# A state-space scan on one core: the product with C written over the states, decays sent three units ahead, and the scan's waits gathered on one instruction

## The chip, the core and the metric

The program runs on one core of a Trainium2 chip. Its engines run side by side, each from its own queue and in that queue's order: PE (TensorE, matrix products), DVE (VectorE), ACT (ScalarE), POOL (GpSimd) and SP (SyncE, which here only issues transfers). The metric is the device time of one execution in microseconds.

## The reference

The reference is two layers. The first adds to x an attention with small latents and a gated feed-forward. The second adds a selective scan (a state-space layer) and a low-rank expert layer. The change lies in the selective scan. For each of 4 sequences of 256 steps, 1024 channels and 16 states per channel:

```python
def step(h, inp):
    x_t, dt_t, B_t, C_t = inp
    dA = jnp.exp(dt_t[..., None] * A)
    dBx = dt_t[..., None] * B_t[:, None, :] * x_t[..., None]
    h = dA * h + dBx
    y = jnp.einsum('bdn,bn->bd', h, C_t)
    return (h, y)
...
y = (ys + D_param[None, :, None] * xc) * jax.nn.silu(z)
return jnp.einsum('bdl,hd->blh', y, out_proj_w)
```

x, z, dt, B and C come from projections of the layer's normalized input, x through a short convolution and a silu, dt through a softplus.

## The kernel before, in words

The order of the work is written out by hand: the program's text is the order of each engine's queue, and a table `put(b, s, f)` says in which unit of the scan a piece of other work is sent. Waits between engines are added from the tiles that instructions read and write.

The first layer takes the first 330 us or so, and its last products (`down`, L469) run on PE until 349.8 us beside the first units of the scan. From there on the scan sets the rhythm. It has 4 batches (stage 0 to 3) of 8 channel blocks of 128 channels, and each block is done in 4 units, one for every 4 of the 16 states: 128 units, numbered `u`. A unit's tiles are [128, 4, 256]: 32 channels by 4 states on the partitions, 4 groups of channels and 256 steps along the free axis. The steps of a unit are:

- `decays(u)`, ACT, L982: four exponentials, exp(dt * A), into a decay tile. There are three such tiles besides the lent ones; unit u takes tile (u - 4) mod 3. They are sent in unit u - 2, at the head of that unit's work on ACT. The tile that they write was last read by the scan of unit u - 3, which is the unit before the one in which they are sent.
- `scan_in(u)`, DVE, L989 and L993: from unit 8 on a no-operation that carries waits (for the decays of u and for POOL's product of u - 2), then bx = B * (dt * x) into PSUM.
- `scan(u)`, DVE, L1008: the recurrence along the steps, into a tile h; then on POOL, L1013, hc = h * C into a tile hc. There are two h tiles and three hc tiles. The first four units use lent tiles (`lent`, L961) in the place of later ones.
- `states_sum(u)`, PE, L1023 and L1025: eight passes that sum hc over the states into ysum. It is sent at the end of unit u + 1, behind that unit's other products on PE. At the end of a block, `take_sum` on ACT (L1030) copies ysum out, and `gate` on POOL (L1033) multiplies it with silu(z).

dt and dt*x reach the layout of the unit through DRAM: POOL makes them (`step_out`, L916 to L920; `step_x`, L927), `send` (L935) stores them, and `spread` (L941) loads them back with four transfers each, as dts for the decays and dus for bx. All of these transfers are on SP's queue, in the text's order, with the weight loads (L623).

The other work of a stage prepares the next batch and ends the one before: on PE the projections px (L759) and pz (L950), the convolution's products (L806), pp (L833), the output products po (L1121) and others; on ACT the copies and scalings of the convolution, two large silu with their table loads (L822, L956, L710), the logarithms and exponentials of dt (`step_exp`, L886 to L889), the inverse root for B, C and dt (L714, L715) and, in two of the stages, ex for the routing (L1070); on DVE a scaling of pp (nrm, L847), statistics, and the routing (from L1060); on POOL the products named above and the sums of the convolution (L813). In unit 4 ACT also does a silu of z (L956) and the scaling of the next batch (xnt, L735), which PE transposes (L743).

## Time and profile before

| what | value |
| --- | --- |
| median of 3 runs | 840.59 us (839.35 to 841.75) |
| the profiled execution's own time | 840.18 us |
| its span | 838.4 us |
| TensorE clock granted, mean | 0.953 |
| busy: PE, DVE, ACT, POOL | 750.9, 654.6, 554.2, 496.9 us |
| decays (L982), one of four | 501 ns, 504 of them |
| hc (L1013) | 2324 ns, 130 of them |
| scan (L1008) | 2235 ns, 129 of them |
| bx (L993) | 1232 ns, 128 of them |

The mean of a row mixes its shapes; the full-sized scan has a median of 2286 ns and the full-sized hc one of 2358 ns. In the trace, "idle before" is the time for which an engine had nothing to do ahead of an instruction, and the name after it is what ended that wait. A wait for several things is put down to the one that came last by the profile. PE's ends are modelled. In the lines of a timeline the columns are start, duration, engine, line and operation, then output and inputs with their sizes.

### The profile page before, as it was taken

To read this page: it belongs to the slowest core of one execution; us is meant where nothing else is said; L and a number is where in the kernel's file an instruction comes from. 1 tells how busy PE (TensorE), PEld (TensorE's weight loads), DVE (VectorE), ACT (ScalarE), POOL (GpSimd) and SP (SyncE) were. 2 spreads that over 40 slices of the span, in tenths; PEclk is the share of its full clock that TensorE was granted. 3 is DMA by queue.
4 is the path that set the end of the run, shared out by engine and by line. 5 is a ranking of instruction groups with operands and counts; after the bars stand their busy time and mean duration, and the time that the engine had idled before them with its cause. 6 is when DMAs were issued, how large, how long until landed. Compare 5 with 4: busy or idle time off the path is not lost.

```text
span 838.4 us, 11286 instructions
## 1 busy us (share of the span) xinstructions
PE 750.9 (90%) x3846; PEld 429.6 (51%) x3846; DVE 654.6 (78%) x604; ACT 554.2 (66%) x1124; POOL 496.9 (59%) x389
## 2 busy tenths in 40 slices
PE   4999999999999999999887999897899987876985
PEld 2665545666555676666543456444457544322331
DVE  4486756288644535797899999988999999999996
ACT  4335564435556277699895898687898787865661
POOL 3133232001343333678878799769799769798775
PEclk9799999999999999999999899989999989988898
DMA  7233332001222322454593544433554443443400
GB/s 226 63 101 106 96 101 63 1 1 38 76 76 79 115 57 64 149 141 126 130 217 109 160 150 115 126 91 105 144 165 114 112 110 92 119 114 120 113 26 25
DMA packets 68644, 86.72 MB, mean 103 GB/s; under 512 B 12221, under 2 KB 52169, under 8 KB 68458
## 3 DMA queue, kind: packets, MB, share of 16 engines
q1 hardware_dynamic: 58794, 65.81, 29.0%
q0 software_dynamic: 9072, 18.35, 7.8%
q10 hardware_dynamic: 720, 1.84, 0.6%
q8 instruction: 30, 0.49, 0.3%
q14 instruction: 28, 0.23, 0.1%
HBM read 66.58 MB, written 10.22 MB: 92 GB/s over the span
## 4 chain that ended last, share of the span: by engine, by line
PE 45%; DVE 23%; POOL 12%; ACT 9%; issue 5%; DMA 5%; SPq 1%; POOLq 0%; ACTq 0%; DVEq 0%
DVE h L1008 11%; POOL hc L1013 8%; PE pg L444 6%; DVE bx L993 6%; PE pu L444 5%; PE po L469 5%; PE av L397 4%; ACT decay L982 3%; PE po L1121 2%; PE px L759 2%; DMA dus<-dud 2%; PE scT L386 2%; DVE mpl L354 2%; PE ysum L1025 2%; DMA dts<-dtd 2%
## 5 line engine op out<-in xcount | busy, mean ns | idle before, releaser
L1013 POOL TENSOR_TENSOR hc<-h,cr 128x1024 f32<-128x1024 f32 (+1 forms) x130 | 301.9, 2324 | 80.5 <-DVE h L1008 70.4
L1008 DVE TENSOR_TENSOR_SCAN h<-decay,bx 128x1024 f32<-128x1024 f32 (+1 forms) x129 | 288.1, 2235 | 8.5 <-PE po L469 3.6
L982 ACT ACTIVATE decay<-dts,aneg 128x255 f32<-128x255 f32 x504 | 213.6, 501 | 52.8 <-DVE h L1008 38.2
L993 DVE TENSOR_TENSOR bx<-brow,dus 128x1024 f32<-128x1024 f32 x128 | 157.7, 1232 | 24.2 <-ACT decay L982 9.3
L1025 PE MATMUL ysum<-hc,stack 128*32 128x256 f32 x1024 | 88.4, 417 | 39.3 <-POOL hc L1013 39.3
L456 POOL TENSOR_TENSOR hlo<-g,hhi 128x512 fp32r<-128x512 f32 x28 | 35.8, 1280 | 115.0 <-ACT hhi L455 115.0
L354 DVE TENSOR_REDUCE mpl<-sc 128x4 f32<-128x1024 f32 x64 | 76.7, 1220 | 22.8 <-PE sc L352 21.3
L427 POOL DMA_DIRECT2D wgu<-in_wgu x56 | 31.1, 555 | 96.0 <-PE pg L444 95.0
L388 ACT ACTIVATE pe<-scT 128x1024 f32<-128x1024 f32 x64 | 64.0, 1023 | 22.9 <-PE sc L352 14.3
L1121 PE MATMUL po<-ow,xc 128*128 128x512 f32 x128 | 72.4, 671 | 5.3 <-POOL xc L1033 4.9
L1025 PEld LDWEIGHTS ysum<-hc,stack 128*32 128x32 f32 x1024 | 21.2, 111 | 99.1 <-POOL hc L1013 69.7
L950 PE MATMUL pz<-xn1T,w_in 128*128 128x256 f32 x256 | 69.3, 419 | 0.0
L759 PE MATMUL px<-xn1T,w_in 128*128 128x256 f32 x256 | 61.0, 383 | 0.4 <-ACT sz L956 0.3
L950 PEld LDWEIGHTS pz<-xn1T,w_in 128*128 128x128 f32 x256 | 50.2, 205 | 19.8 <-issue 11.6
L759 PEld LDWEIGHTS px<-xn1T,w_in 128*128 128x128 f32 x256 | 47.5, 190 | 13.1 <-issue 3.1
L452 DVE SCALAR_TENSOR_TENSOR g<-g,pg 128x512 f32<-128x512 f32 x28 | 19.2, 687 | 43.0 <-ACT g L451 43.0
L444 PE MATMUL pg<-xhi,wgu 128*128 128x512 f32 x112 | 49.7, 443 | 1.0 <-ACT xhi L244 1.0
L469 PE MATMUL po<-wd,hhi 128*128 128x512 f32 x112 | 49.2, 439 | 0.0
L444 PE MATMUL pu<-xhi,wgu 128*128 128x512 f32 x112 | 47.5, 424 | 0.8 <-DVE g L454 0.8
L455 ACT CAST hhi<-g 128x512 fp32r<-128x512 f32 x28 | 17.3, 619 | 45.8 <-DVE g L454 45.8
L444 PE MATMUL pg<-xlo,wgu 128*128 128x512 f32 x112 | 44.9, 401 | 0.7 <-DVE xlo L251 0.7
L444 PE MATMUL pu<-xlo,wgu 128*128 128x512 f32 x112 | 44.6, 398 | 0.0
(237 smaller groups left out, 1276.8 us busy)
## 6 DMA issues: line engine op xcount, KB each, us to landing
dts<-dtd SPq DMA_DIRECT2D x124, 128.0 KB, 2.8
dus<-dud SPq DMA_DIRECT2D x124, 128.0 KB, 3.0
wgu<-in_wgu POOLq DMA_DIRECT2D x56, 256.0 KB, 2.7
w_in<-in_inz SPq DMA_DIRECT2D x16, 512.0 KB, 4.7
w_in<-in_inx SPq DMA_DIRECT2D x14, 512.0 KB, 4.4
dtd<-dt SPq DMA_DIRECT2D x15, 256.0 KB, 2.3
dud<-du SPq DMA_DIRECT2D x15, 256.0 KB, 2.3
wd<-in_wd POOLq DMA_DIRECT2D x7, 512.0 KB, 3.5
```

Of the source, the lines that this page charges most:

```text
L354: nc.vector.tensor_reduce(mpl2[b % 2][:, qb, 2 * hp : 2 * hp + 2, 16 + 2 * gq : 18 + 2 * gq], sc.rearrange("p i (f k) -> p i f k", f=2), A ...
L388: nc.scalar.activation(pes[b, k][:, 2 * t : 2 * t + 2, :], sc, AF.Exp)
L444: mm(ps, lhsT=wgus[i][:, hc, :], rhs=xs[j][:, hc, :], start=(hc == 0 and j == 0), stop=(hc == HC - 1 and j == 1))
L469: mm(po, lhsT=hids[th][j][:, m, i * P : (i + 1) * P], rhs=wd[:, m, :], start=False, stop=(m == MC - 1 and j == 1))
L759: mm(px[:, i, :], lhsT=w[:, i, hc, :], rhs=xns[b][:, hc, :], start=(hc == 0), stop=(hc == HC - 1))
L950: mm(pz[:, i, :], lhsT=w[:, i, hc, :], rhs=xns[b][:, hc, :], start=(hc == 0), stop=(hc == HC - 1))
L982: made["da", u] = nc.scalar.activation(da[:, k, 1:], live["dts", b, c][:, k, 1:], AF.Exp, scale=aneg[:, c, k, g : g + 1])
L993: nc.vector.tensor_tensor(bx, brow[g // 2][:, g % 2, :].unsqueeze(1).to_broadcast([P, NG, S]), live["dus", b, c], ALU.mult)
L1008: nc.vector.tensor_tensor_scan(h[:, n].rearrange("p n t -> p (n t)"), da[:, n].rearrange("p n t -> p (n t)"), bx[:, n].rearrange("p n t -> ...
L1013: made["hc", u] = (nc.vector if k == NG - 1 else nc.gpsimd).tensor_tensor(hc[:, n], h[:, n], crows[b][:, g, :].unsqueeze(1).to_broadcast([ ...
L1025: mm(ysum[k * NB : (k + 1) * NB, :], lhsT=stack, rhs=hc[:, k, :], start=False, stop=(g == NU - 1))
L1121: mm(live["po", b, i], lhsT=xcs[b][:, c, i * P : (i + 1) * P], rhs=late_w["ow"][:, c, :], start=False, stop=(c == DC - 1))
```

## The change

It has three parts.

1. POOL's product with C is written over h, and the hc tiles are gone: four h tiles in the place of two h and three hc. The no-operation ahead of bx waits for the product of unit u - 4 and for PE's sum of unit u - 4, where it waited for the product of unit u - 2. The tiles lent to the first four units are fewer.
2. There are four decay tiles besides the lent ones where there were three, and the decays of a unit are sent three units ahead of it where it was two. The first unit of a batch stays two ahead, and nothing is sent by the new rule before unit 3: units 5 and 6 are both sent in unit 3, unit 7 in unit 4.
3. The no-operation of the first unit of each block also waits for the four transfers of dus, for which bx itself waited.

```diff
-        for i in range(NG):
-            nc.sync.dma_start(t[i * NB : (i + 1) * NB], src)
+        made[n, b, c] = [nc.sync.dma_start(t[i * NB : (i + 1) * NB], src) for i in range(NG)]
...
-    lent = {
-        "d": ("d", "w_in", "d", "w_in"), "h": ("w_in", "u", "e", "u"),
-        "hc": ("w_in", "lw", "w_in", "lw"),
-    }
+    lent = {"d": ("d", "w_in", "d", "w_in"), "h": ("w_in", "lw", "e", "u")}
+    ahead = 3
...
-            da = decay[(u - 4) % 3]
+            da = decay[(u - 4) % (ahead + 1)]
...
             i = nc.vector.engine_nop()
-            for n in (("da", u), ("hc", u - 2)):
-                tc.add_manual_dep(i.ins, made[n].ins.name, early, reason="the scan's waits")
+            first = made["du", b, c] if g == 0 else []
+            for j in (*first, made["da", u], made["hc", u - 4], made["sum", u - 4]):
+                tc.add_manual_dep(i.ins, j.ins.name, early, reason="the scan's waits")
...
-            h, hc = lend("h", u), lend("hc", u)
+            h = lend("h", u)
         else:
-            h = act.tile([P, NG, S], F32, tag="h", name="h", bufs=2)
-            hc = act.tile([P, NG, S], F32, tag="hc", name="hc", bufs=3)
+            h = act.tile([P, NG, S], F32, tag="h", name="h", bufs=4)
...
             made["hc", u] = (nc.vector if k == NG - 1 else nc.gpsimd).tensor_tensor(
-                hc[:, n], h[:, n],
+                h[:, n], h[:, n],
...
-        live["hc", u] = hc
+        live["hc", u] = h
...
-            mm(ysum[k * NB : (k + 1) * NB, :], lhsT=stack, rhs=hc[:, k, :],
-               start=False, stop=(g == NU - 1))
+            made["sum", u] = mm(ysum[k * NB : (k + 1) * NB, :], lhsT=stack, rhs=hc[:, k, :],
+                                start=False, stop=(g == NU - 1))
...
-        decay_tile(act)
-        decay_tile(act)
+        for _ in range(ahead):
+            decay_tile(act)
...
+    due = {}
+    for v in range(5, total):
+        due.setdefault(max(v - ahead + (v % PER == 0), 3), []).append(v)
     for u in range(total + 2):
...
-        if 3 <= u < total - 2:
-            decays(u + 2)
+        for v in due.get(u, ()):
+            decays(v)
```

## The prediction

> **What bounds the kernel now.** I read the stretches first (engine totals for the four batches), then VectorE's waits, the rows of the scan's four steps, and last the timelines of all engines around each wait. Stage b is batch b of the scan: units 32b to 32b+31, a unit being bx, scan, hc and ysum of one quarter of the states. Unit numbers count the L993 rows from the first one at 327.42 us.

> Stretches of the kernel before (per engine: busy us and instructions):

> ```profile
> 327.00:467.00 140.00, 122.55 (x655) 77.66 (x654) 122.97 (x102) 114.57 (x259) 108.99 (x71) 0.94 0.59 150
> 467.00:591.00 124.00, 112.09 (x566) 60.95 (x567) 113.87 (x70) 101.44 (x231) 103.51 (x63) 0.94 0.44 122
> 591.00:715.00 124.00, 112.23 (x596) 63.09 (x594) 117.45 (x90) 102.38 (x234) 103.28 (x62) 0.97 0.43 121
> 715.00:840.00 125.00, 94.83 (x430) 36.20 (x426) 114.01 (x71) 71.67 (x154) 92.80 (x52) 0.89 0.30 83
> ```

> VectorE (the third figure of busy time) leads, but PE, ACT and POOL are at 82 to 91% in the first three stages, so a stall of VectorE is often only the shadow of another engine that is full. VectorE's own waits from 327 us on (total us, times, longest):

> ```profile
> DVE bx L993 <- ACT decay L982: 9.3, 8, 4.1
> DVE bx L993 <- POOL hc L1013: 6.7, 10, 1.1
> DVE h L1008 <- PE po L469: 3.6, 1, 3.6
> DVE bx L993 <- ACT pad L771: 3.2, 1, 3.2
> ```

> The last one, at unit 16, is POOL's too: ACT's copy was long done, and hc of unit 14 ended 0.24 us before that bx. Floor of a unit, from the rows of page part 5: bx 1.232 + scan 2.286 + two gaps of 0.035 = 3.59 us. Over the 128 units, gaps before bx sum to 28.3 us, of which the floor is 5 and some 3 lie around small VectorE work; the removable waits are 9.1 (decays, eight times) and 10.4 (POOL, unit 16 and seven small ones included): 19.5 us.

> [...] the ten POOL waits are for h, which has two. [...] where the nop let go late, bx came 0.20 us after hc's end and not 0.04. [...]

> **The change, part by part.**

> *C in place, four h.* Five tiles become four. POOL's product in place: the halves L918 (in place) and L927 (not) both took 1.27 us, so 0; at most the row's own spread, 40 ns for each of some eight products in a POOL-bound end, 0.3 us either way. The nop's wait for hc(u-2) becomes hc(u-4), which every hc in the trace meets (the latest ended 7.8 us after its scan; 10.8 are allowed). Added is PE's ysum(u-4). Behind the waiting nop stands all of VectorE; POOL and PE wait for that. It must be done three units and a gap after its scan: 3 x 3.59 + 0.04 = 10.8 us. Latest ysums now: unit 17 at 10.97, 49 at 10.53, 13 at 10.38, 88 at 9.70. PE is late there by its own queue, so each microsecond that VectorE gains before comes back here.

> *Decays three ahead.* No instruction is added; a group of four (1.65 us) enters ACT's queue one unit earlier and still waits for scan(u-1). So, in time, each ACT slot keeps its place and holds the next unit's group: 3.6 us more margin once the queue is running. dts must land a slot earlier: the least margin by slot is 0.1 us (unit 16) and -0.2 (unit 24), with VectorE not waiting there; at the batch starts the order stays two ahead. To get ahead, one extra group is put in at unit 4:

> ```profile
> 349.86 3.30 ACT L982 ACTIVATE decay<-dts,aneg 128x255 f32<-128x255 f32 x8 [7.28 <-PE po L469]
> 353.18 1.28 ACT L956 ACT_TABLE_LOAD   x1
> ```

> ```profile
> 357.25 1.82 PE L743 MATMUL pt<-cst,xnt 128*128 128x128 f32 x8 [1.92 <-ACT xnt L735]
> ```

> The program's order has twelve decays where these eight stand. ACT then has 0.2 us idle until 402.9, and PE waits only for ACT (1.9, 1.0, 0.3, 0.5). So both run 1.65 us later up to the silu near 410 us and the product behind it. Bounds: 0 (absorbed) to 1.65; I take 1.65. The one added clearing on POOL is 0.1 us, under PE's po.

> *dus waits on the nop.* Four DMA waits per channel block move ahead one instruction. They were exposed only where POOL held the nop (0.16 x 6 = 1 us, counted in the 10.4); alone the part is worth 0 to 1 us, I take 0 beside the first. The previous scan (2.29 us) covers them on VectorE's queue; uncovered they would cost 0.16 at 31 block starts, 5 us. The SP queue keeps its order.

> *Loans in units 0 to 3.* Two fewer w_in tiles are lent, so SP's weight loads near 347 to 361 us may go sooner; no px or pz in that stretch waits for a load, so 0. Late, they would hold px, but they can only be earlier.

> **Stage by stage.**

> *Stage 0.* Up to unit 20 the waits go (10, 13, 14, 16), but VectorE runs into ysum and into dus(20), which POOL's full queue sends. Deciding are:

> ```profile
> 417.14 0.64 PE L1025 MATMUL ysum<-hc,stack 128*32 128x256 f32 x8
> ```

> ```profile
> 418.89 0.42 ACT L715 ACTIVATE rs<-rs 64x256 f32<-64x256 f32 x1
> ```

> ```profile
> 419.38 1.23 DVE L993 TENSOR_TENSOR bx<-brow,dus 128x1024 f32<-128x1024 f32 x1
> ```

> This ysum (17) ends at 417.8 + 1.65 = 419.4 and releases bx(21), which started at 419.38 anyway. rs ends at 419.3 + 1.65 = 420.96; nrm (0.47) and the scan follow at 421.4, against 420.9 before: 0.5 lost. POOL's wait at unit 29 goes: +0.8. Stage 0: +0.25 of the 9 us of stalls.

> *Stage 1.* The wait at 38 goes (0.74) and POOL, which idled 0.72 for that scan, moves with it; PE idles 0.79 for POOL at 507 us and follows. After that PE and POOL have no hole until 531 us, so the waits at 43 to 51 (1.5 us) end in ysum(49) at 543.4 - 0.7 and nrm at unit 53; the gain stands at 0.74. Then the largest wait:

> ```profile
> 567.16 1.23 DVE L993 TENSOR_TENSOR bx<-brow,dus 128x1024 f32<-128x1024 f32 x1 [4.12 <-ACT decay L982]
> ```

> ```profile
> 557.23 1.70 ACT L982 ACTIVATE decay<-dts,aneg 128x255 f32<-128x255 f32 x4
> ...
> 565.33 1.70 ACT L982 ACTIVATE decay<-dts,aneg 128x255 f32<-128x255 f32 x4
> ```

> Unit 58's group moves into the slot at 557.2, 59's into 565.3. bx(59) can start at 567.0 - 0.7 + 0.1 = 566.4 against 570.75: gain 4.35; the wait at 61 makes it 5.15. POOL is full from 561.8 (waiting for ACT) with one hole of 0.72, so it moves by 0.74 + 0.72 = 1.46, and dus(64), landed at 588.38, by as much: bx(64) at 587.0 against 591.17. Stage 1: +4.1.

> *Stage 2.* Waits of 2.65 us in all, but the routing at unit 89 starts when ACT's ex lands:

> ```profile
> 684.09 0.20 DVE L1060 TENSOR_REDUCE w<-ex 128x4 f32<-128x32 f32 x1 [0.83 <-ACT ex L1070]
> ```

> ACT and PE move only by the 0.24 of unit 70, so 0.25 is left there. After it unit 93 (0.77) and 96 (0.14) go: +1.2.

> *Stage 3.* VectorE alone, 115 of 115 us; 0.38 at unit 102 and 0.08 at 112 go: +0.5. The tail is unchanged.

> Sum 0.25 + 4.1 + 1.2 + 0.5 = 6.0 us. The profiled execution took 840.18 (span 838.4 and 1.8 around it), so 834.2; the median shown is 0.4 higher, and I say 834.3.

> **The rivals.**

> *All stalls go* (chance 0.06): 19.5 us, 820.7. For it: every stall named is addressed. Against: PE has no hole in 507 to 531 us, ACT none in 350 to 403.

> *The opening push is absorbed and the full queues yield* (0.22): stage 0 gains 1.5 + 0.8, stage 1 the 5.15, stage 2 its 2.65, stage 3 0.5: 10.6 us, 829.6. For it: PE's ends are modelled, so its holes may be larger than shown. Against: rs and ex are ACT's, not modelled.

> *The gains are eaten, within 0.3%* (0.12): bx(59) waits, because ACT's slots after unit 55 hold one group more than I count (1.65, and its push on POOL 1.0), stage 2 gives 0.3 and stage 3 nothing: 0.25 + 1.45 + 0.3 = 2.0 us, 838.2, or 838.6 beside the median. For it: ACT is full from 557 to 574 us. Against: the slot count above.

> *PE's ysum becomes the pace* (0.05), slower. At units 30, 62 and 94 two groups stand in one unit. If that pushes PE by 1.65 each time as at unit 4, lags are 12.6, 12.2 and 11.3 us in stages 0 to 2; past the allowed 10.8 every excess (1.8, 1.4, 0.6) is lost, and what the other waits give back is spent waiting: 840.2 + 3.8 = 844. It decides where a lag passes 10.8 us and VectorE has no other stall to trade. Against: the unit before has no group, so ACT's slots only swap.

> That the decays are not earlier can't be: the program's order has them so.

> **How the numbers follow.** The likeliest (0.55) is 834.3, its own range 831.5 to 837. The 80% range is 827.5 to 839: it leaves out the first rival, the fastest tail of the second, and the slower one. A measurement tells about 0.3% (2.5 us) from no change; below 838.1 is faster: 0.55 + 0.22 + 0.06 = 0.83. Within 0.3%: 0.12. Slower: 0.05.

> **What would show it.** Right: no wait of bx for POOL's hc; bx waiting for PE's ysum at units 17 and 21 (1 to 2 us each) and at 53; dus a wait at 20 and 64; unit 58 free and 59 waiting under 1.5 us for ACT; twelve decays in a row near 350 us and the transposes of xnt 1.65 us later; stage 1 shorter by 4 us, stage 0 by less than 1. Wrong: ysum waits over 3 us in sum, stage 0 shorter by 2 or more, or ACT still ahead of bx at 58.

## The result, and the profile after

| | kernel before | changed kernel |
| --- | --- | --- |
| median | 840.66 us (839.35 to 842.86, 8 runs) | 837.25 us (835.19 to 838.26, 8 runs) |
| ratio to before, 95% interval | | 0.9952 (0.9940 to 0.9965) |
| profiled execution, its span | 840.18, 838.4 us | 836.09, 834.3 us |
| start of the first bx | 327.42 us | 324.83 us |
| TensorE clock granted, mean | 0.953 | 0.952 |

The kernel is faster by 3.4 us; 6.0 to 6.3 were forecast. In a second series it was 836.35 us against 840.70, ratio 0.9947 (0.9931 to 0.9962).

Below "gain" always counts from the bx of unit 0: the start of a step minus the start of bx of unit 0, kernel before less the other. That is needed because the two heads, in which nothing was changed, differ by 2.6 us; over the thirteen profiles of this study the first bx started at 324.8 to 327.6 us.

VectorE's waits in the scan of the changed kernel (total us, times, longest):

```profile
DVE bx L991 <- PE ysum L1022: 5.4, 5, 2.4
DVE bx L991 <- POOL xc L1030: 3.8, 1, 3.8
DVE h L1005 <- PE po L469: 3.6, 1, 3.6
DVE bx L991 <- POOL h L1010: 2.6, 1, 2.6
DVE w L1057 <- ACT ex L1067: 2.5, 1, 2.5
DVE nrm L847 <- ACT rs L715: 2.4, 2, 1.2
...
DVE bx L991 <- ACT decay L979: 1.7, 1, 1.7
...
DVE bx L991 <- DMA dus<-dud: 1.3, 2, 0.9
```

The removable waits of before, ACT's decays and POOL's hc, are gone. In their place stand PE's sums, dus and the two ends of ACT's chains, rs and ex: the queues that were full all along. Three names mislead: the 3.8 at unit 20 is dus (the second profile names its transfer, 3.6 us); the 2.6 at unit 53 is the sum of unit 49, which ended 0.20 us before that bx (the second profile: ysum, 2.3 us); and the 1.7 at unit 13 is the sum of unit 9, which ended 0.20 us before that bx, when the decays had been done for 2.6 us.

The large wait of stage 1 is where the gain is made. In the kernel before, unit 58 waited 4.12 us. These are bx and scan of unit 58 and bx of unit 59 in the changed kernel, and then bx of unit 64, with which stage 2 begins:

```profile
562.26 1.23 DVE L991 TENSOR_TENSOR bx<-brow,dus 128x1024 f32<-128x1024 f32 x1
563.53 2.29 DVE L1005 TENSOR_TENSOR_SCAN h<-decay,bx 128x1024 f32<-128x1024 f32 x1
565.85 1.23 DVE L991 TENSOR_TENSOR bx<-brow,dus 128x1024 f32<-128x1024 f32 x1
...
586.25 1.23 DVE L991 TENSOR_TENSOR bx<-brow,dus 128x1024 f32<-128x1024 f32 x1 [0.90 <-DMA dus<-dud]
```

By stages the gain, from two profiles of the changed kernel against the first of before (stage 3 up to the end of the span):

| stage | forecast | measured, profile 1 and 2 |
| --- | --- | --- |
| 0 | +0.25 | -1.07, -1.23 |
| 1 | +4.1 | +3.40, +3.62 |
| 2 | +1.2 | -1.26, -0.23 |
| 3 | +0.5 | +0.43, +0.36 |
| sum | 6.0 | 1.5, 2.5 |

The kernel before, profiled again, took 1.0 us more for its scan than in its first profile, so 1.5 to 3.6 us is what the profiles of the scan give; the medians give 3.4 and 4.4.

Stage 0 goes wrong at its start. First ACT's push of decays, then PE beside it, in the changed kernel:

```profile
347.26 4.90 ACT L979 ACTIVATE decay<-dts,aneg 128x255 f32<-128x255 f32 x12 [7.34 <-PE po L469]
352.18 1.28 ACT L955 ACT_TABLE_LOAD   x1
```

```profile
356.25 1.97 PE L743 MATMUL pt<-cst,xnt 128*128 128x128 f32 x8 [3.52 <-ACT xnt L735]
...
360.02 2.07 PE L872 MATMUL pdt<-nrm,dtw 32*128 32x256 f32 x4
...
363.03 3.10 PE L759 MATMUL px<-xn1T,w_in 128*128 128x256 f32 x8
```

Twelve decays stand in a row, and the transposes of xnt wait 3.52 us where they waited 1.92: the forecast push of 1.65 us (measured 1.60 on ACT). Not forecast are the last two lines: products of a size that take 1.13 and 1.99 us elsewhere took 2.07 and 3.10. The stretches of 3.4 us show why; the seventh figure is PE's granted clock (us, then PE, PEld, DVE, ACT and POOL busy, clock, DMA share, GB/s):

```profile
351.50:354.90 3.40, 1.24 (x8) 0.66 (x4) 3.12 (x3) 3.35 (x5) 1.31 (x2) 1.00 0.82 191
...
358.30:361.70 3.40, 3.40 (x14) 1.42 (x13) 3.27 (x2) 3.40 (x10) 2.87 (x2) 0.50 0.43 134
361.70:365.10 3.40, 3.40 (x14) 1.92 (x14) 3.33 (x3) 3.40 (x10) 2.36 (x1) 0.50 0.54 140
365.10:368.50 3.40, 3.40 (x22) 2.34 (x21) 3.33 (x3) 3.34 (x5) 2.38 (x1) 0.97 0.00 0
```

In the records of the clock it is at half from 355.1 to 365.3 us, 10.2 us; in the kernel before this took 3.4 us (357.8 to 361.2). My theory after this, then untested: the push costs 1.6 us by its length and nearly as much again by PE's clock, and clock losses in stages 1 and 2 take more. The rivals: the sum of u-4 and dus are the limit and the push is harmless; or the push counts, but the clock doesn't.

### The profile page after: what moved, and what is told of

It is laid out like the page before. It is cut to its first block, busy times and chain, and to the rows that moved or that the text cites. A ratio compares the mean times of both kernels' runs of the same rounds, so it can differ in the third digit from the quotient of the medians.

```text
span 834.3 us, 11274 instructions
## 1 busy us (share of the span) xinstructions
PE 749.0 (90%) x3846; PEld 429.7 (51%) x3846; DVE 654.7 (78%) x604; ACT 554.0 (66%) x1124; POOL 496.9 (60%) x390
## 3 DMA queue, kind: packets, MB, share of 16 engines
q10 hardware_dynamic: 720, 1.84, 0.7%
## 4 chain that ended last, share of the span: by engine, by line
PE 47%; DVE 26%; ACT 9%; POOL 7%; issue 5%; DMA 4%; SPq 1%; ACTq 0%; POOLq 0%; DVEq 0%
DVE h L1005 13%; DVE bx L991 7%; PE pg L444 6%; PE pu L444 5%; PE px L759 4%; POOL h L1010 4%; PE av L397 4%; PE px L806 3%; PE po L469 3%; PE ysum L1022 3%; PE scT L386 2%; PE po L1118 2%; PE pz L949 2%; PE pp L833 2%; ACT decay L979 2%
## 5 line engine op out<-in xcount | busy, mean ns | idle before, releaser
L1010 POOL TENSOR_TENSOR h<-h,cr 128x1024 f32<-128x1024 f32 (+1 forms) x130 | 302.0, 2326 | 72.3 <-DVE h L1005 60.5
L991 DVE TENSOR_TENSOR bx<-brow,dus 128x1024 f32<-128x1024 f32 x128 | 157.7, 1232 | 19.0 <-PE ysum L1022 5.4
L1022 PE MATMUL ysum<-h,stack 128*32 128x256 f32 x1024 | 87.0, 412 | 37.9 <-POOL h L1010 37.9
L1022 PEld LDWEIGHTS ysum<-h,stack 128*32 128x32 f32 x1024 | 21.0, 111 | 97.3 <-POOL h L1010 66.2
L469 PE MATMUL po<-wd,hhi 128*128 128x512 f32 x112 | 49.2, 439 | 0.0
```

Of the source, the lines that this page charges most:

```text
L469: mm(po, lhsT=hids[th][j][:, m, i * P : (i + 1) * P], rhs=wd[:, m, :], start=False, stop=(m == MC - 1 and j == 1))
L991: nc.vector.tensor_tensor(bx, brow[g // 2][:, g % 2, :].unsqueeze(1).to_broadcast([P, NG, S]), live["dus", b, c], ALU.mult)
L1010: made["hc", u] = (nc.vector if k == NG - 1 else nc.gpsimd).tensor_tensor(h[:, n], h[:, n], crows[b][:, g, :].unsqueeze(1).to_broadcast([P ...
L1022: made["sum", u] = mm(ysum[k * NB : (k + 1) * NB, :], lhsT=stack, rhs=hc[:, k, :], start=False, stop=(g == NU - 1))
```

## The experiments

The gain over the first profile of before, at the bx of the units named, with the half clock (us) in three places: after the push (units 4 to 11), at pp (units 16 to 21), and around unit 50 (from 1 us ahead of bx of 49 to bx of 54).

| kernel | u22 | u32 | u52 | u54 | u64 | u84 | u89 | u127 | half clock: push, pp, u50 |
| --- | --- | --- | --- | --- | --- | --- | --- | --- | --- |
| before, 2nd profile | -0.54 | -0.53 | -0.69 | -0.70 | -0.30 | -0.31 | -0.32 | -1.04 | 3.4, 3.4, 3.4 |
| changed | -1.84 | -1.07 | 1.18 | -1.79 | 2.33 | 4.25 | 0.22 | 1.55 | 10.2, 3.4, 6.8 |
| changed, 2nd profile | -1.99 | -1.23 | 1.02 | -1.71 | 2.39 | 4.31 | 1.32 | 2.64 | 10.2, 3.4, 6.8 |
| product_only | 0.01 | 0.75 | 1.17 | 1.16 | 1.99 | 1.83 | 1.82 | 1.28 | 3.4, 3.4, 3.4 |
| decays_only | -0.43 | -0.45 | 0.62 | -0.63 | 0.80 | 1.77 | 0.77 | 1.30 | 3.4, 3.4, 3.4 |
| late_lead | 0.18 | 0.91 | 3.16 | 3.23 | 6.97 | 8.89 | 6.43 | 7.76 | 3.4, 3.4, 0 |
| early_dus | 0.19 | 0.92 | 3.16 | 0.75 | 4.70 | 6.62 | 4.10 | 5.43 | 3.4, 3.4, 3.4 |
| warm_pe | -1.60 | -0.83 | 1.42 | -0.02 | 3.65 | 4.35 | 0.75 | 2.08 | 0, 6.8, 3.4 |
| warm_both | -1.80 | -1.05 | 1.19 | -1.59 | 2.59 | 4.50 | 1.41 | 2.73 | 0, 0, 6.8 |
| warm_short | -0.91 | -0.15 | 2.10 | -0.75 | 3.34 | 5.26 | 2.23 | 3.56 | 3.4, 0, 6.8 |
| stage0_order | 2.38 | 3.13 | 5.38 | 3.87 | 7.71 | 9.63 | 7.11 | 8.43 | 3.4, 3.4, 3.4 |
| all_order | 2.60 | 3.35 | 5.60 | 4.91 | 6.85 | 8.77 | 4.65 | 5.98 | 3.4, 3.4, 6.8 |

### The two kernels again

Labels after_again and before_again, no edit.

> The changed kernel once more, beside the others on one chip. Both theories: 837.2 us, 0.995 of the kernel before, stage 0 (bx of unit 0 to bx of unit 32) 140 us, with some 10 us of half clock on PE right after unit 4.

> The kernel before once more, for how far one profiled execution stands for others. Theory (stages repeat, and what differs between executions is where PE's clock halves): stage 0 138.5 to 139.3 us, stage 1 124 to 125.5, stage 2 123 to 124.5, stage 3 123.7, each longer where there is more half clock; bx of unit 0 at 324.8 to 327.6 us. Rival (one profile tells nothing of others): stages differ by 2 us or more with the same stretches of half clock.

Measured: 836.35 us (835.88 to 837.85), ratio 0.9947 (0.9931 to 0.9962), stage 0 140.19 us, half clock 10.2 us after the push; and, before again, 839.38 us in one run, stages 139.49, 124.56, 123.53 and 124.45 us (the first 0.2 and the last 0.7 us over what I expected), first bx at 325.57. Units repeat to some 0.2 us where the clock's stretches lie alike, and differ by 1 us where they don't: at unit 89, 0.22 with 9.9 us of half clock since unit 85 and 1.32 with none. So a gain at a unit can be compared between profiles, if the clock is read beside it.

### No push at the opening

Label late_lead: the lead of three begins at unit 30.

```diff
-        due.setdefault(max(v - ahead + (v % PER == 0), 3), []).append(v)
+        due.setdefault(v - 2 if v < 30 else v - ahead + (v % PER == 0), []).append(v)
```

> The changed kernel, but the lead of three units begins only at unit 30 (units below that are sent two units ahead), so that no third group of decays stands in the queue of ACT at unit 4. Theory (the opening push idles PE for 3.5 us ahead of the transposes of xnt, PE's clock goes to half for 10 us, and stage 0 loses both): stage 0 takes 136.8 to 137.5 us in place of 140.0, half clock after unit 4 at most 3.4 us, time 834.2 to 834.8. Rival 1 (stage 0 lost its gain to the new wait for the sum of u-4 and to dus, not to the push): stage 0 139.5 to 140, time 837. Rival 2 (only the 1.65 us of the push count, not the clock): stage 0 138.4, time 835.6.

Measured: stage 0 138.04 us, half clock after unit 4 3.4 us, 836.46 us (832.18 to 838.00), ratio 0.9942 (0.9921 to 0.9963). Stage 0 is 2.0 us shorter than the changed kernel's, so the push does harm, and rival 1 falls. But it is not as short as I expected (136.8 to 137.5), and it lies nearer to rival 2 (138.4, the push without the clock), so this run doesn't tell the two apart. At unit 20 VectorE waits about as long as in the changed kernel (3.84 us there), now for the decays, which at a lead of two come late.

```profile
415.73 1.23 DVE L991 TENSOR_TENSOR bx<-brow,dus 128x1024 f32<-128x1024 f32 x1 [4.05 <-ACT decay L979]
```

The median is no better than the changed kernel's 836.35. Here and in early_dus, which has the same waits in stage 0, five executions of thirteen had a mean clock of 0.954 or more, and took 832.2 to 834.7 us; the other eight took 835.0 to 838.0. Of the fourteen executions of the changed kernel one reached 0.954, and the fastest took 835.19 us. So in these runs what is won over the changed kernel shows only where PE's clock stays up.

### Is it PE's clock?

Labels warm_pe, warm_both and warm_short: products whose results are overwritten, in PE's idle time ahead of the transposes of xnt, and (in the last two) ahead of pp.

```diff
         pt = psmm.tile([P, HC, P], F32, tag="mm", name="pt")
+        for _ in range(14 if (b, i) == (1, 0) else 0):
+            mm(pt[:, 0:2, :].rearrange("p a b -> p (a b)"), lhsT=ident, rhs=xns[0][:, 0, :], start=True, stop=True)
...
             live["pp"] = psmm.tile([P, 2, S], F32, tag="mm", name="pp")
+            for _ in range(14 if b == 1 else 0):
+                mm(live["pp"][:, 1, :], lhsT=ident, rhs=xns[0][:, 0, :], start=True, stop=True)
```

(warm_pe has the first loop alone; warm_short has 7 in the place of 14.)

> The changed kernel, with 14 more products on PE (128x128 by 128x256, into the tile that the transposes of xnt fill, overwritten by them), sent ahead of the first transposes of xnt in unit 5, where PE idles 3.5 us; the push of the decays stays. Theory (the half clock after that idle time costs 1.4 us of the 3.0 that PE's and ACT's queues lose there): no half clock from 352 to 366 us, pdt x4 back to 1.2 us and px x8 to 1.9, stage 0 138.4 to 138.9 us, time 835.7 to 836.2. Rival (the clock is harmless, the push alone counts): stage 0 140.0, time 837.2. Second rival (the added products delay the transposes): stage 0 over 140, time over 837.2.

> The changed kernel with the 14 added products on PE at unit 5 of warm_pe, and 14 more ahead of the first product of pp (unit 17), where PE idles 3.9 us; they write parts of tiles that are overwritten afterwards. Theory (the push costs ACT's and PE's queues 1.6 us; what came on top of it, 1.4 us in the changed kernel and 1.1 us in warm_pe, is half clock, at 355 us in the one and from 410 us on in the other): no half clock from 350 to 420 us, rs 1.6 us later than in the kernel before or less (counted from bx of unit 0), and stage 0 138.6 to 139.4 us against 140.0 to 140.2. Rival (the rest of the loss is queueing, not clock): rs 2.7 us late or more, stage 0 139.8 or more. Either way the time is 835 to 837, since later stages are the same.

> warm_both with the right size: seven added products at each of the two places and not fourteen (a product took 0.45 us in warm_both, so fourteen ran 6.3 us and pushed pp by 2.3 us; seven are 3.2 us, inside the idle 3.5 and 3.9 us). Theory (the clock is what came on top of the push): no half clock from 350 to 420 us, silu and take_sum of ACT 1.6 us late as in decays_only, pp x16 3.7 us in place of 5.3, so rs 0 to 0.6 us late against 3.0 in the changed kernel, and stage 0 138.2 to 139.0 us. Rival (queueing): rs 1.6 us late or more, stage 0 139.4 or more.

Measured: warm_pe 835.84 us, ratio 0.9940 (0.9920 to 0.9959), stage 0 139.79; warm_both 837.69, ratio 0.9957 (0.9941 to 0.9973), stage 0 140.01; warm_short 836.03, ratio 0.9949 (0.9930 to 0.9967), stage 0 139.11. None of the three expectations of stage 0 was met, and the rival's figures, those of queueing without the clock, came out in warm_both (stage 0 of 139.8 or more, rs 2.7 us late or more) and, for rs, in warm_short (1.6 or more). So by the end of the stage these three don't show the clock's part. Along ACT's queue they say more. How late it was against before, counted from bx of unit 0, at four places (with their time in the kernel before):

| | table load of sz, 353.2 us | copy of ysum, 372.3 | silu of xc (L822), 408.6 | rs, 418.9 |
| --- | --- | --- | --- | --- |
| changed, two profiles | 1.60, 1.61 | 2.98, 2.83 | 3.01, 3.15 | 3.01, 3.15 |
| warm_pe | 1.60 | 1.61 | 1.72 | 2.76 |
| warm_both | 1.59 | 1.60 | 1.63 | 2.96 |
| warm_short | 1.60 | 2.05 | 2.41 | 2.08 |
| decays_only | 1.59 | 1.60 | 1.59 | 1.59 |

With the clock kept up after the push ACT is 1.6 us late at the copy of ysum and not 2.9: the other 1.3 were half clock. In warm_pe a stretch of 6.8 us at half (410.0 to 416.8) then takes 1.0 back. In warm_both my added products did it: they ran far past the idle time and held pp.

```profile
408.96 6.31 PE L835 MATMUL pp<-xn1T,cst 128*128 128x256 f32 x28 [0.69 <-ACT xc L820]
415.20 3.67 PE L837 MATMUL pp<-xc,xpw 128*64 128x256 f32 x16
```

Fourteen products are 28 records here; I had counted one each. The first fourteen ran over too, 6.31 us where PE idled 3.52, so that the transposes began 2.6 us later than in the changed kernel (counted from bx of unit 0); PE had made that up by the copy of ysum. In warm_short, with the right size, a stretch of 3.4 us at half still came (361.9 to 365.3).

The clean comparison wasn't planned as one: decays_only (next), which sends ACT and PE the changed kernel's work in the same order. It happened to have 3.4 us of half clock after the push, and all of ACT stayed 1.59 us late up to rs. PE after its push:

```profile
356.89 1.92 PE L743 MATMUL pt<-cst,xnt 128*128 128x128 f32 x8 [3.52 <-ACT xnt L735]
...
360.63 1.13 PE L872 MATMUL pdt<-nrm,dtw 32*128 32x256 f32 x4
...
362.25 1.99 PE L759 MATMUL px<-xn1T,w_in 128*128 128x256 f32 x8
```

The wait is the same 3.52 us, the products after it have their full speed, and at unit 22 the loss is 0.43 us, the 0.5 that I had forecast for a push alone. In the changed kernel it is 1.84 and 1.99. The rest, 1.4 to 1.6 us, goes with the clock.

### One part without the other

Label product_only: four h tiles and the product in place, decays two ahead in three tiles, dus waited for by bx. Label decays_only: all of the change, but the old wait for POOL.

```diff
-    ahead = 3
+    ahead = 2
...
-            first = made["du", b, c] if g == 0 else []
-            for j in (*first, made["da", u], made["hc", u - 4], made["sum", u - 4]):
+            for j in (made["da", u], made["hc", u - 4], made["sum", u - 4]):
...
-        due.setdefault(max(v - ahead + (v % PER == 0), 3), []).append(v)
+        due.setdefault(v - 2, []).append(v)
```

```diff
-            for j in (*first, made["da", u], made["hc", u - 4], made["sum", u - 4]):
+            for j in (*first, made["da", u], made["hc", u - 2], made["sum", u - 4]):
```

> The kernel before with only the product with C written over the states (four h tiles, the wait for the product of u-4 and the sum of u-4); decays two units ahead with three tiles, dus waited for by bx as before. Theory (the product's part takes away the waits for POOL, most of which come back as waits for PE's sum or dus; the gain of the change lies in the decays of stage 1): stage 0 137 to 138 us, stage 1 123.5 to 124.2 with a wait of 4 us for the decays at unit 58 still there, stage 2 122.8 to 123.3, stage 3 123.4, time 838 to 839. Rival (POOL's waits were the loss, the decays only their shadow): unit 58 waits under 2 us and the time is 836.5 or less.

> The changed kernel with the old wait for POOL put back: the no-operation waits for the product of u-2 and not of u-4 (the sum of u-4 stays). So the decays are three ahead, but what four h tiles give is taken away. Theory (the decays of unit 58 carry the gain; the waits for POOL are mostly the shadow of dus and of the sums): the POOL waits at 13 to 16 and 43 to 51 come back with 3 to 5 us in sum, stage 0 140 to 140.5, stage 1 121.5 to 122.5, stage 2 124 to 125, stage 3 123.4, time 837 to 838.5. Rival (the gain needs both parts, VectorE cannot use the early decays if POOL holds it): stage 1 over 123.5, time 839.5 to 841.

Measured: product_only 837.77 us, ratio 0.9965 (0.9953 to 0.9977), stages 138.21, 123.55, 122.82, 125.05; decays_only 839.40 us, ratio 0.9986 (0.9973 to 0.9998), stages 139.40, 123.54, 123.49, 123.37. The first went as expected to 0.2 us, but for 1.5 us lost in stage 3 at unit 102, where the decays now come last. The second was worse than I expected: its rival, that the gain needs both parts, had stage 1 (over 123.5), and the time lies 0.1 us under the rival's range. VectorE's waits of the two, product_only first:

```profile
DVE bx L990 <- ACT decay L979: 12.5, 8, 4.1
```

```profile
DVE bx L991 <- POOL h L1010: 15.8, 12, 3.3
```

Take one wait away and the other grows, from 9.3 to 12.5 us and from 6.7 to 15.8. At unit 58 the decays alone give 2.45 us and both parts give 4.1. Product and lead give 2.9 and 1.2 us by these ratios, each known to 1 us or so, 4.1 together, against 4.0 and 4.4 for the change; that the parts simply add is not shown more closely than that. In product_only bx itself waits for dus, and at the block starts where nothing else is late the gap is still 0.03 to 0.04 us: beside the first part, the third is worth nothing that can be seen. (In the kernel before, bx came 0.04 us after the end of hc at the units held by POOL within a block, and 0.24 us after it (0.20 in the forecast) at the block starts 16, 44, 48, 76 and 80.)

### What holds unit 20, and a faster version

Labels early_dus, stage0_order and all_order, each built on the one before it, the first on late_lead.

```diff
-            put(b, 4 * c - 4 + o, spread, "du", b, c)
+            put(b, 4 * c - 4 + o - (b == 0 and c == 5), spread, "du", b, c)
```

```diff
-        due.setdefault(v - 2 if v < 30 else v - ahead + (v % PER == 0), []).append(v)
+        due.setdefault(v - 2 if v < 19 else v - ahead + (v % PER == 0), []).append(v)
...
-            put(b, 18, pp_mm, nxt, 1)
+            (put_end if b == 0 else put)(b, 18, pp_mm, nxt, 1)
...
-            put_mid(b, 21, pp_norm, nxt)
+            (put_late if b == 0 else put_mid)(b, 21, pp_norm, nxt)
```

(all_order has put_end and put_late in every batch.)

> late_lead with one thing more: the load of dus for unit 20 is sent in unit 16 and not in unit 17, so that on the SP queue it stands ahead of the store of dt*x for units 24 to 31 (which waits for POOL until 408 us). Theory (the wait of 4 us at unit 20 is the store in front of the load on SP, not POOL's product nor the decays): the four loads go out at about 405 us in place of 408.7, bx of 20 waits under 1.5 us, and stage 0 becomes shorter by 0.7 to 1.2 us than late_lead's 138.0, the scan of unit 21 then waiting for nrm; time 835.5 or less. Rival 1 (the decays of unit 20, the named releaser, are the limit): bx of 20 still waits 3.5 us or more. Rival 2 (nrm takes all of it): the wait moves whole to unit 21 and stage 0 stays at 138.

> early_dus with three things more, all in stage 0: the lead of three begins at unit 19 (two groups stand in unit 16, where ACT idles 2.3 us for PE), the second half of pp goes behind the sum of unit 17 on PE, and nrm behind the scan of unit 21 on VectorE. Theory (the 4 us at unit 20 have three gates in a row, none alone enough: dus behind the store on SP, the decays of unit 20 behind the silu on ACT, then the sum of 17 and nrm at unit 21): bx of 20 waits under 1 us, bx of 21 under 1.5, stage 0 135.0 to 136.3 us against 138.0, time 832 to 834. Rival (a fourth gate, or the work of ACT and PE behind it comes later by as much): stage 0 137.5 or more, time 835 to 836.

> stage0_order with the second half of pp behind the sum, and nrm behind the scan, in stages 1 and 2 too (units 49 and 53, 81 and 85). Theory (those two gates cost 2.5 us at unit 53 and 1 to 2.4 at 85 whenever PE's clock is at half before them): no wait for the sum at 53 and 85, stage 1 118.5 to 120 us with half clock too, stage 2 122.5 to 123.5, time 831 to 833.5. Rival (where the clock is full nrm comes 1.2 us later and ACT's and PE's queues with it, which the decays or ex give back): a new wait for ACT after 85 or at 89, stage 2 124 or more, time no better than stage0_order.

Measured: early_dus 834.86 us, ratio 0.9926 (0.9904 to 0.9949), stage 0 138.04, the same as late_lead. The load of dus did go out earlier, at 403.4 us, and the wait did not move: rival 1 was right, the decays hold it. (The median is within what I expected, 835.5 or less, but not by what I expected.)

```profile
414.01 1.23 DVE L991 TENSOR_TENSOR bx<-brow,dus 128x1024 f32<-128x1024 f32 x1 [4.04 <-DMA dts<-dtd]
```

(What is named is the transfer of dts, but ACT's group for units 20 and 21 ran from 412.2 on; its first half ended just before this bx.) With the other gates opened too, stage0_order took 831.08 us (830.20 to 834.52), ratio 0.9900 (0.9876 to 0.9925), stage 0 135.82. Units 20, 21 and 22 of it:

```profile
409.70 1.23 DVE L991 TENSOR_TENSOR bx<-brow,dus 128x1024 f32<-128x1024 f32 x1
410.97 2.29 DVE L1005 TENSOR_TENSOR_SCAN h<-decay,bx 128x1024 f32<-128x1024 f32 x1
414.81 1.23 DVE L991 TENSOR_TENSOR bx<-brow,dus 128x1024 f32<-128x1024 f32 x1 [1.55 <-PE ysum L1022]
416.08 2.29 DVE L1005 TENSOR_TENSOR_SCAN h<-decay,bx 128x1024 f32<-128x1024 f32 x1
418.57 0.48 DVE L847 SCALAR_TENSOR_TENSOR nrm<-pp,lnw,rs 64x256 f32<-64x256 f32 x1 [0.21 <-ACT rs L715]
419.44 1.23 DVE L991 TENSOR_TENSOR bx<-brow,dus 128x1024 f32<-128x1024 f32 x1 [0.40 <-PE ysum L1022]
```

The 4 us at unit 20 are gone, 1.55 of them return at 21, and the scan of 21 no longer stands behind nrm. ACT's chain pays 0.62 us (rs), less than VectorE gains. This is the fastest version of the study, and its interval lies wholly below that of the changed kernel. Doing the same in stages 1 and 2 gains nothing more: all_order 831.81 us, ratio 0.9905 (0.9880 to 0.9930), stage 2 124.86 us as its rival had it. The wait for the sum at unit 53 shrinks only from 1.10 to 0.71 us, and nrm comes later, ACT's and PE's queues with it: unit 59 waits 2.13 us for its decays, where it had waited 0.14, stage 1 takes 121.30 us where I expected 120 at most, and the routing waits for ex.

```profile
DVE w L1057 <- ACT ex L1067: 4.3, 1, 4.3
```

Stage 2 also had 10.2 us of half clock there in all_order against 6.8 in stage0_order, and unit 50 had 6.8 against 3.4, so how much of these waits is nrm and how much clock isn't settled.

## Why the prediction was right in kind and too large in size

*The waits, and where they go.* Right. No bx waits for POOL's product; at units 17 and 21 bx waits 2.40 and 1.02 us for PE's sum, at 53 for the sum of 49 (2.3 to 2.6 us), at 20 and 64 for dus (3.8 and 0.9), unit 58 is free, and 59 doesn't wait at all. Wrong by the forecast's own mark was one: the waits for sums come to 5.4 us by name and 9.7 with units 13 and 53, where over 3 was to count against it. The places were right and the lengths weren't.

*The product in place: nothing.* Right. POOL's full-sized product takes 2362 ns on the mean after and 2359 before. That VectorE would lose nothing by it was my estimate; the full-sized scan has a median of 2286 ns in both kernels, and bx one of 1232 ns.

*The decays' slots.* Right: the wait at unit 58 is gone whole, a step of 4.10 us, 0.80 follows at 61 (0.80 forecast), and the limit by dus at 64 takes 0.8 us (1.0 forecast). The forecast's 4.35 counted from the stage's start, with the 0.74 of its first half in it; counted so, unit 59 stood at 3.4 and 3.6.

*Stage 0, the term "both run 1.65 us later".* Half right: 1.60 was the push, passed on to rs as forecast, and it alone costs 0.43 at unit 22 (decays_only). Mis-sized was PE's part: I took PE as waiting for ACT and then at its pace, but after a wait of 3.5 us its clock fell for 10.2 us and not for 3.4, which made rs 3.0 to 3.15 us late and not 1.6. That is 1.3 to 1.5 us of the shortfall. That the clock makes the difference rests on decays_only, which has the push and lacks the long stretch; the three warm runs, made to test it, did not show it by the stage's time.

*Stage 1, "the gain stands at 0.74".* At unit 54 it stood at -0.72 and -0.48 from the stage's start. In the changed kernel's profiles PE was at half clock for 6.8 us around unit 50 where before had 3.4. Over the runs the step of the gain from unit 52 to unit 54 is +0.07 us with no half clock there (late_lead), -1.4 to -2.4 with 3.4 us (warm_pe, stage0_order, early_dus), -2.7 to -3.0 with 6.8 (the changed kernel twice, warm_both, warm_short). The order of work is the same in all seven behind unit 30; the clock differs, and the loss goes with it. Only product_only and before itself, where VectorE comes later to unit 53, lose nothing to 3.4 us.

PE's queue shows the price: from the end of its wait of 3.07 us near unit 51 to the end of the sum of unit 49 it took 6.64 us in late_lead, 8.16 to 8.25 in the profiles with 3.4 us of half clock, and 9.42 to 9.65 in those of the seven with 6.8. (The 2.4 is early_dus; it had another 3.4 us at half from 478.5 us on, and came to that wait 0.9 us later.) The forecast had carried over the clock of the profile that it was read from. Where the half clock around unit 50 was 3.4 us, as there, unit 54 stood at 0.81, 0.74 and -0.17 from the stage's start (warm_pe, stage0_order, early_dus); with none at 2.32. From the forecast 4.1 the longer stretch took 0.5 to 0.7 at the stage's end; with no half clock there the stage gained 6.1 us, so that 4.1 is no limit of the order of work either.

*Stage 2, "0.25 is left there".* This step failed by its own reasoning. I let the stage's gain begin at zero for all engines alike, as if PE and ACT entered it with the 4.1 us that VectorE had. They didn't. In the second profile VectorE stood at 2.39 at unit 64, but ACT's copies of xn1T after it (L751) at 0.43, and rs of unit 85 and ex of unit 89 at 1.32, where VectorE's gain then ended up: 4.31 at unit 84, 1.32 at unit 89. PE, near the end of stage 1, waits for POOL, and is then busy without a hole to 609 us:

```profile
583.59 0.98 PE L1022 MATMUL ysum<-h,stack 128*32 128x256 f32 x8 [1.86 <-POOL h L1010]
584.50 3.29 PE L949 MATMUL pz<-xn1T,w_in 128*128 128x256 f32 x8
```

POOL is itself full from 560 us on (busy for 27.7 of the 28 us up to 588), which I had used for dus(64) and not for PE. In late_lead and stage0_order 1.4 to 1.5 us lie between VectorE at unit 64 (6.97 and 7.71) and ACT's L751 after it (5.55 and 6.21), where the changed kernel has 2.0; they lack its stretch of 3.4 us at half clock near 584 us, so some 0.5 us of the step may be clock. This account of stage 2 is read from the traces; no experiment moved PE or POOL there. In the first profile of the changed kernel a stretch of 10.2 us at half clock, from 675.9 us on, took a further 0.9 (rs stood at 1.16, ex at 0.22):

```profile
665.15 0.48 DVE L847 SCALAR_TENSOR_TENSOR nrm<-pp,lnw,rs 64x256 f32<-64x256 f32 x1 [1.19 <-ACT rs L715]
...
681.28 0.20 DVE L1057 TENSOR_REDUCE w<-ex 128x4 f32<-128x32 f32 x1 [2.50 <-ACT ex L1067]
```

So the stages' gains don't add: what VectorE had won in stage 1 and in units 64 to 84 was given back at units 85 and 89, because the queues that feed those had not moved as far.

*Stage 3.* Right: 0.43 and 0.36 for 0.5.

*The sum.* Against the second profile the 6.0 lose 1.5 in stage 0, 0.5 in stage 1, 1.4 in stage 2 and 0.1 in stage 3, and 2.5 are left. That the medians differ by 3.4 and 4.4 is not explained unit by unit; the first profile of before had a scan 1.0 us shorter than its second, and the heads vary by 2.7 us. Two of the four stages lost where a gain was forecast, and stage 1 carried the whole.

*The rival "the gains are eaten".* By the number it came nearer than the forecast: 837.25 us lies just above the range given to the likeliest case (831.5 to 837), inside the 80% range, and 1.4 us under this rival's 838.6. Its mechanism isn't what happened: bx of unit 59 does not wait for ACT, and stage 3 kept its gain.

*The rival "PE's ysum the pace".* It is the mechanism that came nearest to the truth in stage 0: the sums' lags passed what the no-operation allows, at units 13, 17 and 21. Its price was too high, since the two-group units 30, 62 and 94 cost nothing that shows; the opening alone did.

The loans in units 0 to 3 were not tried alone, but cost nothing that shows: up to unit 9 each bx of late_lead, which has them, starts within 0.06 us of where it did before, counted from bx of unit 0. Open stays in part why PE's clock took longer to come back after the same wait of 3.5 us in the changed kernel than in decays_only; the last section has what the records say.

## What to carry to other kernels

Sending work of one engine earlier needs one extra group somewhere; put it where that engine has idle time of its own (unit 16 here, tried together with two other moves) and not where the others wait for it (unit 4). A gain belongs to an engine at a place: before adding it to the next stage's, look whether the queue that ends the next stage's wait has moved too. A wait often has several gates behind one another, of which the trace names the last; opening one shows the next. At unit 20 opening the first gave nothing (stage 0 of 138.04 us with and without), and opening all gave 2.2 us.

## What the runs showed of the hardware

*What told more was PE's busy time in each piece of the grid.* Cut along it, the thirteen profiles have 1677 pieces at full clock in the scan. After all 74 in which PE was busy for less than 0.40 of the piece the next was at half; after the 1297 with 0.75 or more none was; after the 306 between, 78 were. (In the first profiles of the two kernels alone: all of 13, none of 196, and 11 of 46. Busy is what the profile shows, with modelled ends.) Take PE's wait of 3.07 us near unit 51, first in early_dus, then in late_lead (columns as above: PE's busy time is the second figure, its clock the seventh):

```profile
529.73:533.15 3.42, 0.35 (x2) 0.30 (x2) 3.35 (x3) 3.39 (x6) 2.52 (x2) 1.00 1.00 214
533.15:536.56 3.41, 3.41 (x15) 1.23 (x14) 3.34 (x3) 3.41 (x10) 2.87 (x3) 0.50 0.58 153
```

```profile
528.80:532.21 3.41, 1.79 (x11) 0.45 (x10) 3.34 (x3) 3.38 (x4) 3.41 (x2) 1.00 0.84 234
532.21:535.63 3.42, 1.97 (x14) 0.99 (x15) 3.35 (x3) 3.41 (x8) 2.31 (x2) 1.00 0.75 155
```

In early_dus nearly the whole wait lies in one piece, and the next is at half. In late_lead two pieces share it, and the clock stays up. From the end of the wait to the end of the sum of unit 49 PE then took 8.22 us in the one and 6.64 in the other, with the same work in the same order. The push is alike: its wait of 3.52 us fills one piece in decays_only (PE busy for 0.09 us) and is shared by two in the changed kernel (1.09 and 2.22 us), the second of them already at half. Pieces at half with PE busy for less than 0.8 were followed by another at half in all 45 cases. But the third half piece of the changed kernel came after one in which PE was busy throughout, and of 168 half pieces with 0.9 or more 145 were followed by full clock; what sets the other 23 apart stays open.

*Time and clock went together.* Over 75 executions of the kernel before the span correlates with the mean granted clock at -0.82: 2.7 us longer for each 0.01 of clock less. A change of half a per cent in this kernel is measured through that.

*A product of f32 128x128 by 128x256 stands in the trace as two records and took 0.45 us* on a PE at full clock (warm_both from 408.96 us: 28 records in 6.31 us for fourteen products). One record there is 0.38 us long, and the next starts 0.22 us after it did.
